# Where the last batch's x_proj is made: at the end of the first pass, or among the pieces of the scan pass

## The chip, the cores and the metric

The kernel runs on one core of one Trainium2 chip. The metric is the device time of one execution in microseconds (us); the median of a few runs counts. The profile is one execution, recorded instruction by instruction. Its engines are PE (matrix products and transposes, results in PSUM), PEld (PE's weight loads), DVE (vector), ACT (scalar, activation functions), POOL and SP, which here only starts transfers. Every engine works through its own list of instructions in order and waits on semaphores for the others.

## The reference, cut to what matters

A batch of 8 images of 64 x 64 points with 96 channels goes through a state-space block, a linear attention block and a feed-forward block. The change lies in the first of them:

```python
xz = jnp.einsum('bhwc,ec->bhwe', x, in_proj_w)         # 96 -> 384, split into xin, z
xc = jax.nn.silu(conv3x3_depthwise(xin) + conv_b)      # 192 channels: u
xs = concatenate([x_hwwh, flip(x_hwwh)], axis=1)       # 4 directions: rows, columns, both reversed
x_dbl = jnp.einsum('bkdl,kcd->bkcl', xs, x_proj_weight)   # x_proj: 192 -> 6 + 16 + 16
dts, Bs, Cs = split(x_dbl)
delta = jax.nn.softplus(einsum(dts, dt_projs_weight) + bias)
h = h * jnp.exp(d_t * A) + (d_t * u_t) * b_t           # the scan over L = 4096, 16 states
y = sum_n(h * c_t)
```

`x_proj` gives, for each point and direction, the 6 values that delta is made of, the 16 factors B and the 16 factors C. The scan of a batch can't start before that batch's x_proj is there.

## The kernel before, in words

There are three passes, each with tile pools of its own in SBUF and PSUM, which the next pass takes over; arrays go from pass to pass through HBM (`u_d`, `z_d`, `xd_d`, `b_d`, `dt_d`, `y_d`). The 8 batches are handled in four pairs. Of the 192 channels of two batches, three chunks of 128 are made (`chunk_rows`): the first 128 channels of each batch, and the last 64 of both together.

**First pass** (`pass1`). For each batch: statistics, projection (`projection`), a depthwise convolution of nine taps on DVE (`convolution`) into a tile `u` of 128 x 4096, SiLU on ACT. `u` is stored twice in `u_d`: row by row as it is (2 MB for a chunk) and, by way of ACT's copies `ut` (four of 128 x 1024, two buffers), column by column. `x_projection(b, o, q)` then makes x_proj of a batch for 512 points, for both directions of one order `o` at once: two products `px` of `u` with the weights `w_xp` (line 504), a copy from PSUM into `xd` (four buffers) by ACT, and a store into `xd_d`. There are 16 such units per batch. In the last batch every second copy is DVE's. `split` cuts the B and dt parts of `xd_d` into three bf16 parts (a load `bq`, ACT and POOL steps, two stores); for batches below `LATE` = 5 this is done in the first pass, for the others among the scans (`late_split`).

**Scan pass** (`pass2`). 192 pieces: pair, chunk, direction, quarter of 1024 points. `prepare` loads `xdt`, `xb` and `u` of a piece (for the very first piece on POOL's queue, for all others on SP's), and makes delta, `du` and transposes through the `wide` tiles in PSUM, of which there are three. Then for each of 16 states n: the decay `da` (ACT), the product `dbu` in a `wide` tile (by PE from ACT's or POOL's `x`, or from PE and a DVE product), the scan `h` (DVE, 2.3 us), and for every two states a product with C by POOL (`c`, loaded by SP into one of six buffers) and a sum by PE (`acc`).

**Third pass** (`pass3`): norm, gate, attention, feed-forward.

In each pass the order of instructions on each engine is written by a planner, `weave`. Units of work are generators that name the engine, an estimated cost and a delay; the planner takes, step by step, what can begin first, the lower rank where two can begin at once. It keeps `room` units of a kind open. `InOrder` (line 91 in the profile, for nearly every instruction) fixes that order. So a unit that is added shifts the order of others around it. The constants:

```python
LATE = 5
room = {"c": 6, "da": 3, "h": 3, "x": 3, "wide": 3, "xg": 1, "ud": 1, "acc": 1}
```

Of the kernel before, what the change touches and what calls it, by code (L numbers as in the profile page):

```python
# [33 lines left out]
F32 = mybir.dt.float32  # L34
# [8 lines left out]
P = 128  # L43
# [3 lines left out]
NXD = R + 2 * N  # L47
# [8 lines left out]
NS = 3  # L56

LATE = 5
GRP = 512
NG = L // GRP  # L60
RPG = GRP // WW
# [38 lines left out]
@with_exitstack  # L100
def vss_attn_ffn_kernel(ctx: ExitStack, tc: tile.TileContext, g: dict, out: bass.AP):
    nc = tc.nc
    consts = ctx.enter_context(tc.tile_pool(name="consts", bufs=1))
    dram = ctx.enter_context(tc.tile_pool(name="scratch", bufs=1, space=DRAM))

    ident = consts.tile([P, P], F32, name="ident")
    make_identity(nc, ident)
    mhalf = consts.tile([P, NBLK], F32, name="mhalf")
    nc.vector.memset(mhalf, -0.5)


    u_d = [[dram.tile([DI, L], F32, name=f"u_d{b}_{o}") for o in range(2)] for b in range(NB)]

    y_d = [[dram.tile([L, DI], F32, name=f"y_d{b}_{o}") for o in range(2)] for b in range(NB)]
    z_d = [dram.tile([DI, L], F32, name=f"z_d{b}") for b in range(NB)]
    xd_d = [[dram.tile([2 * NXD, L], F32, name=f"xd_d{b}_{o}") for o in range(2)] for b in range(NB)]

    b_d = [[dram.tile([2, NS, N, L], BF16, name=f"b_d{b}_{o}") for o in range(2)] for b in range(NB)]
    dt_d = [[dram.tile([2, NS, R, L], BF16, name=f"dt_d{b}_{o}") for o in range(2)] for b in range(NB)]

    engines = [InOrder(tc, e) for e in (nc.tensor, nc.vector, nc.scalar, nc.gpsimd)]
    fixed, load_dt_w = scan_constants(tc, g, consts, dram, ident)
    pass1(tc, g, load_dt_w, ident, mhalf, engines, u_d, z_d, xd_d, b_d, dt_d)
    pass2(tc, g, ident, engines, fixed, u_d, xd_d, b_d, dt_d, y_d)
    pass3(tc, g, ident, mhalf, engines, y_d, z_d, out)


# [138 lines left out]
def pass1(ctx, tc, g, load_dt_w, ident, mhalf, engines, u_d, z_d, xd_d, b_d, dt_d):  # L266
    nc = tc.nc
    pe, dve, act, pool = engines
    sp = InOrder(tc, nc.sync)
# [22 lines left out]
    conv_w = wp.tile([P, 2, 9], F32, name="conv_w")  # L292
    conv_b = wp.tile([P, 2, 1], F32, name="conv_b")

    w_xp = wp.tile([P, 3, 2, P], F32, name="w_xp")
    pool.memset(w_xp, 0.0)

    def later_loads():
# [191 lines left out]
    def x_projection(b, o, q):  # L490
        pair, j = b // 2, b % 2
        yield "u", pair, j
        yield "u", pair, 2
        px = None
        for ty, u in ((0, us[pair, j]), (1 + j, us[pair, 2])):
            end = yield ("pe", 0.62, 0.4) if px else ("pe", 0.62, 0.4, pxs)
            if px is None:
                px, slot = ps_px.tile([P, GRP], F32, name="px", tag="px"), pxs.taken
            if o == 0:
                src = u[:, q * GRP : (q + 1) * GRP]  # L500
            else:
# [10 lines left out]
        (dve.tensor_copy if by_dve else act.copy)(dst, src)  # L512
# [10 lines left out]
    for pair in range(NB // 2):  # L523
        batches = (2 * pair, 2 * pair + 1)
        for b in batches:
            units += [("stats", statistics(b, q)) for q in range(NG)]
            units.append(("norm", group_norm(b)))
            units += [("proj", projection(b, q)) for q in range(NG)]
        for c in ORDER:
            units.append(("conv", convolution(pair, c)))  # L530
        for b in batches:
            for o in range(2):
                units += [("xproj", x_projection(b, o, q)) for q in range(NG)]
                if b < LATE:
                    units += [("split", after(("xd", b, o), split((act, pool, sp), two, 4.4, xd_d[b][o], *w))) for w in splits(b, o, b_d, dt_d)]
# [3 lines left out]


@with_exitstack
def pass2(ctx, tc, g, ident, engines, fixed, u_d, xd_d, b_d, dt_d, y_d):
    nc = tc.nc
    KB = 2 * NS * N
    a_neg, dsum, dt_b, dt_w, sel, sel2 = fixed
# [27 lines left out]
    def prepare(at):  # L573
# [265 lines left out]
    for at, (pair, c, k, pc) in enumerate(pieces):  # L839
        by_act, by_pool = WAYS[c // 2]  # L840

        def add(kind, lead, unit, n=0):
            units.append((kind, at * N + n - lead, unit))

        add("prep", 8, prepare(at))
        for n in range(N):
            if n % 2 == 0:
                add("c", 12, load_c(at, n // 2), n)
            add("da", 2, decay(at, n), n)
            if n in by_act:  # L850
# [12 lines left out]
    units += [("split", 5 * N * (i + 1), late_split(*which)) for i, which in enumerate(last)]  # L863
    weave(units, {"prep": 1, "c": 1, "da": 2, "x": 1, "xg": 1, "dbu": 2, "scan": 2, "carry": 1, "term": 1, "sum": 1, "acc": 1, "split": 1}, done)


@with_exitstack
# [297 lines left out]
```

## Time and profile before

| | |
|---|---|
| median of 3 runs | 10121.8 us (10119.1 to 10127.6) |
| span of the profiled execution | 10130.1 us (its only listed time) |
| busy: DVE, ACT, POOL, PE | 9551 (94%), 9187 (91%), 8990 (89%), 7527 (74%) us |
| first convolution-free moment of DVE, last `px` product | 643.6 us, 695.2 us |
| first scan work on DVE | 716.6 us |
| one piece of the scan pass | about 44 to 46 us |
| scan pass | from about 710 to about 9300 us |
| granted clock of PE, mean | 0.906 |

An engine's busy share is a mean over three passes with different limits. In the timeline a line gives the start, the length, the engine and the operation, and in brackets how long the engine had been idle before it and what ended that. A piece's place in time is read here from the start of its product `du` on POOL, which every piece has once.

### The profile page before, as it was taken

What the parts mean: (1) busy time and instruction counts of PE and PEld (TensorE: products, weight loads), DVE (VectorE), ACT (ScalarE), POOL (GpSimd) and SP (SyncE); (2) the same over time, 40 slices, a digit from 0 to 9 for tenths busy, and PEclk for the clock granted to TensorE, in tenths of its full rate; (3) what the DMA queues carried; (4) which work ended last, traced back from release to release, by engine and by line L of the source; (5) the groups of instructions that cost most, each with busy time, mean ns of one, the idle gap of its engine ahead of it and who ended that gap; (6) DMA issues with size and microseconds to landing.
All of it is one profiled execution on the core that took longest, in us unless ns stands there. A gap on an engine that the chain in (4) does not pass through costs nothing.

```text
span 10130.1 us, 152413 instructions
## 1 busy us (share of the span) xinstructions
PE 7527.0 (74%) x52384; PEld 6235.5 (62%) x52384; DVE 9551.4 (94%) x7025; ACT 9186.9 (91%) x20692; POOL 8990.2 (89%) x2911
## 2 busy tenths in 40 slices
PE   7767777777777777777777777777777777776777
PEld 3336666665666666666666666655666666565666
DVE  7869999999999999999999999999999999998887
ACT  5669999999999999999999999999999999997776
POOL 1439999999999999999999999999999999998665
PEclk8889998989998989989999989999989999998887
DMA  5766776789976776799966766899767667998652
GB/s 167 233 205 215 225 236 217 229 210 206 209 219 213 225 218 214 223 211 200 223 211 214 230 212 223 212 205 209 217 213 225 218 212 224 208 203 183 192 151 77
DMA packets 932228, 2111.66 MB, mean 208 GB/s; under 512 B 274603, under 2 KB 422860, under 8 KB 929922
## 3 DMA queue, kind: packets, MB, share of 16 engines
q1 hardware_dynamic: 928650, 2100.57, 74.0%
q8 instruction: 419, 6.86, 0.3%
q14 instruction: 351, 2.88, 0.1%
q0 software_dynamic: 432, 0.94, 0.0%
q10 hardware_dynamic: 2376, 0.40, 0.0%
HBM read 1925.98 MB, written 175.66 MB: 207 GB/s over the span
## 4 chain that ended last, share of the span: by engine, by line
DVE 30%; ACT 29%; issue 15%; PE 13%; POOL 9%; DMA 3%; SPq 1%; DVEq 0%; ACTq 0%; POOLq 0%
DVE h L91 20%; ACT x L91 11%; ACT da L91 10%; POOL c L91 7%; PE acc L91 6%; DVE wide L91 5%; PE wide L91 3%; ACT L91 2%; ACT y L91 1%; POOL xg L91 1%; PE px L91 1%; PE pa L91 1%; ACT delta L91 1%; DMA xd_d<-xd 1%; DVE u L91 1%
## 5 line engine op out<-in xcount | busy, mean ns | idle before, releaser
L91 POOL TENSOR_TENSOR c<-c,h 128x2048 f32<-128x2048 f32 x1536 | 6959.5, 4557 | 300.0 <-issue 139.4
L91 DVE TENSOR_TENSOR_SCAN h<-da,carry,wide 128x1024 f32<-128x1024 f32 x2304 | 5268.3, 2332 | 137.5 <-PE wide L91 36.8
L91 ACT ACTIVATE x<-duT,bT 128x128 f32<-128x128 f32 (+1 forms) x13312 | 3970.8, 369 | 2.0
L91 PE MATMUL acc<-ident,c 128*128 128x128 f32 x24576 | 3439.1, 298 | 571.0 <-POOL c L91 563.3
L91 ACT ACTIVATE da<-delta,a_neg 128x1024 f32<-128x1024 f32 x3072 | 3513.4, 1144 | 316.2 <-DVE h L91 303.1
L91 PEld LDWEIGHTS acc<-ident,c 128*128 128x128 f32 x24576 | 3123.4, 155 | 1005.5 <-POOL c L91 891.2
L91 PE MATMUL wide<-ident,x 128*128 128x128 f32 x10752 | 1560.7, 291 | 645.3 <-DVE h L91 586.4
L91 PEld LDWEIGHTS wide<-ident,x 128*128 128x128 f32 x10752 | 1306.9, 150 | 841.5 <-ACT x L91 399.4
L91 DVE TENSOR_TENSOR_SCAN h<-da,wide 128x1024 f32<-128x1024 f32 x768 | 1712.9, 2271 | 46.2 <-PE wide L91 14.0
L91 DVE TENSOR_TENSOR wide<-du,wide 128x1024 f32<-128x1024 f32 x1280 | 1544.0, 1208 | 39.9 <-PE wide L91 39.6
L91 PE MATMUL wide<-xb,sel 96*128 96x512 bf16 x2560 | 820.5, 404 | 697.4 <-DVE h L91 686.4
L91 POOL TENSOR_TENSOR xg<-duT,bT 128x512 f32<-128x512 f32 (+1 forms) x640 | 894.5, 1414 | 28.3 <-PE wide L91 15.2
L91 PEld LDWEIGHTS <-sel 96*128 96x128 bf16 x2560 | 232.7, 102 | 878.1 <-DVE h L91 626.3
L91 PE MATMUL wide<-ident,xg 128*128 128x128 f32 x3584 | 483.8, 279 | 119.0 <-DVE h L91 116.4
L91 ACT ACT_TABLE_LOAD x386 | 495.2, 1283 | 26.3 <-DMA w_qT<-in_WqT_b 19.5
L91 PEld LDWEIGHTS wide<-ident,xg 128*128 128x128 f32 x3584 | 412.6, 144 | 148.9 <-issue 111.2
L91 POOL TENSOR_TENSOR du<-delta,u 128x1024 f32<-128x1024 f32 x192 | 457.5, 2383 | 7.5 <-ACT delta L91 7.5
L91 DVE SCALAR_TENSOR_TENSOR u<-xpad,conv_w,u 128x4096 f32<-128x4096 f32 x96 | 450.9, 4697 | 1.9
L91 PE MATMUL px<-u,w_xp 128*128 128x512 f32 x512 | 252.7, 633 | 63.4 <-ACT u L91 43.8
L91 POOL TENSOR_TENSOR gt<-gt,zs 128x512 f32<-128x512 f32 x128 | 161.8, 1275 | 132.1 <-ACT gt L91 111.9
L91 ACT COPY y<-acc 128x1024 f32<-128x1024 f32 x192 | 192.6, 1003 | 83.8 <-PE acc L91 83.5
L91 POOL TENSOR_TENSOR bq<-bq,bs 128x512 f32<-128x512 f32 (+1 forms) x48 | 115.1, 2400 | 166.9 <-ACT bs L91 155.1
(142 smaller groups left out, 5987.7 us busy)
## 6 DMA issues: line engine op xcount, KB each, us to landing
c<-xd_d SPq DMA_DIRECT2D x1024, 1024.0 KB
c<-xd_d SPq DMA_DIRECT2D x1024, 512.0 KB
u<-u_d SPq DMA_DIRECT2D x127, 512.0 KB
xdt<-dt_d SPq DMA_DIRECT2D x1146, 36.0 KB
xb<-b_d SPq DMA_DIRECT2D x382, 96.0 KB
u<-u_d SPq DMA_DIRECT2D x128, 256.0 KB
zs<-z_d SPq DMA_DIRECT2D x128, 256.0 KB
y_d<-y SPq DMA_DIRECT2D x24, 1024.0 KB
```

The source lines that it names most:

```text
L91: ins = getattr(self.engine, op)(*args, **kwargs).ins
```

## The change

For batches from `LATE_X` = 7 on, so for the last batch alone, `x_projection` is no longer put into the first pass. In its place, sixteen units `late_x_projection` are put into the scan pass. Each loads 512 points of `u` (or of its column order) back from `u_d` into a tile `ux` (three transfers), makes the two products into a `wide` tile, copies it with ACT into a tile `xd` and stores it in `xd_d`. One such unit is open at a time. The late splits of batch 7 wait for them. `w_xp` lies in a pool of its own that both passes share, so that other tiles of the passes lie at other addresses.

```diff
+LATE_X = 7
...
-    pass1(tc, g, load_dt_w, ident, mhalf, engines, u_d, z_d, xd_d, b_d, dt_d)
-    pass2(tc, g, ident, engines, fixed, u_d, xd_d, b_d, dt_d, y_d)
+    with tc.tile_pool(name="shared", bufs=1) as shared:
+        w_xp = shared.tile([P, 3, 2, P], F32, name="w_xp")
+        pass1(tc, g, load_dt_w, ident, mhalf, engines, w_xp, u_d, z_d, xd_d, b_d, dt_d)
+        pass2(tc, g, ident, engines, fixed, w_xp, u_d, xd_d, b_d, dt_d, y_d)
...
-        by_dve = b == NB - 1 and q % 2 == 1
-        end = yield ("dve" if by_dve else "act"), 0.6 if o == 0 else 0.8
+        end = yield "act", 0.6 if o == 0 else 0.8
...
-            for o in range(2):
+            for o in range(2 if b < LATE_X else 0):
...
+    def late_x_projection(b, o, q):
+
+        yield "scans", 0
+        pair, j = b // 2, b % 2
+        cols = slice(q * GRP, (q + 1) * GRP)
+        yield "sp", 1.8, 4.0
+        ux = one.tile([P, 2, GRP], F32, name="ux")
+        sp.dma_start(ux[:, 0, :], u_d[b][o][0:P, cols])
+        for i in range(2):
+            sp.dma_start(ux[64 * i : 64 * i + 64, 1, :], u_d[2 * pair + i][o][P:DI, cols])
+        yield "pe", 1.5, 0.2, slots["wide"]
+        px, slot = take("wide", [P, T])
+        for i, ty in enumerate((0, 1 + j)):
+            pe.matmul(px[:, 0:GRP], w_xp[:, ty, o, :], ux[:, i, :], start=i == 0, stop=i == 1)
+        end = yield "act", 0.58, 0.2
+        xd = one.tile([2 * NXD, GRP], F32, name="xd")
+        act.copy(xd, px[0 : 2 * NXD, 0:GRP])
+        slots["wide"].release(slot, end)
+        end = yield "sp", 0.7, 3.0
+        sp.dma_start(xd_d[b][o][:, cols], xd)
+        one_more(("xd", b, o), NG, end)
...
     def late_split(b, o, which):
 
         yield "scans", 0
+        if b >= LATE_X:
+            yield "xd", b, o
...
+    late_x = [(b, o, q) for b in range(LATE_X, NB) for o in range(2) for q in range(NG)]
+    units += [("late", 3 * N * (i + 1), late_x_projection(*which)) for i, which in enumerate(late_x)]
     last = [(b, o, w) for b in range(LATE, NB) for o in range(2) for w in splits(b, o, b_d, dt_d)]
     units += [("split", 5 * N * (i + 1), late_split(*which)) for i, which in enumerate(last)]
-    weave(units, {"prep": 1, ..., "acc": 1, "split": 1}, done)
+    weave(units, {"prep": 1, ..., "acc": 1, "late": 1, "split": 1}, done)
```

More of the change, by code (lines that the diff above doesn't have):

```diff
@@ L265, in pass1 @@
 @with_exitstack
-def pass1(ctx, tc, g, load_dt_w, ident, mhalf, engines, u_d, z_d, xd_d, b_d, dt_d):
+def pass1(ctx, tc, g, load_dt_w, ident, mhalf, engines, w_xp, u_d, z_d, xd_d, b_d, dt_d):
     nc = tc.nc
@@ L293, in pass1 @@
     conv_b = wp.tile([P, 2, 1], F32, name="conv_b")
-    w_xp = wp.tile([P, 3, 2, P], F32, name="w_xp")
     pool.memset(w_xp, 0.0)
@@ L511, in x_projection @@
             src, dst = src.rearrange("p (h w) -> p w h", w=RPG), xd.rearrange("p (w h) -> p w h", w=RPG)
-        (dve.tensor_copy if by_dve else act.copy)(dst, src)
+        act.copy(dst, src)
         pxs.release(slot, end)
@@ L541, in pass2 @@
 @with_exitstack
-def pass2(ctx, tc, g, ident, engines, fixed, u_d, xd_d, b_d, dt_d, y_d):
+def pass2(ctx, tc, g, ident, engines, fixed, w_xp, u_d, xd_d, b_d, dt_d, y_d):
     nc = tc.nc
@@ L861, in pass2 @@
         add("acc", 0, take_acc(at), N)
+    late_x = [(b, o, q) for b in range(LATE_X, NB) for o in range(2) for q in range(NG)]
+    units += [("late", 3 * N * (i + 1), late_x_projection(*which)) for i, which in enumerate(late_x)]
     last = [(b, o, w) for b in range(LATE, NB) for o in range(2) for w in splits(b, o, b_d, dt_d)]
     units += [("split", 5 * N * (i + 1), late_split(*which)) for i, which in enumerate(last)]
-    weave(units, {"prep": 1, "c": 1, "da": 2, "x": 1, "xg": 1, "dbu": 2, "scan": 2, "carry": 1, "term": 1, "sum": 1, "acc": 1, "split": 1}, done)
+    weave(units, {"prep": 1, "c": 1, "da": 2, "x": 1, "xg": 1, "dbu": 2, "scan": 2, "carry": 1, "term": 1, "sum": 1, "acc": 1, "late": 1, "split": 1}, done)
 @with_exitstack
```

## The prediction

> **What bounds the kernel now.** I read four views, from wide to narrow. The page's forty slices say where engines rest.
>
> ```profile
> DVE  7869999999999999999999999999999999998887
> ACT  5669999999999999999999999999999999997776
> POOL 1439999999999999999999999999999999998665
> ```
>
> Each slice is 253 us. From the fourth slice to the 36th all three are nine tenths busy or more: that is the scan pass. The third slice (507 to 760 us) holds the seam between the passes, which the change edits. The busy time by stretches takes it apart (columns: stretch, its length, then busy us and instructions of PE, PEld, DVE, ACT, POOL, the granted clock, the DMA share, GB/s).
>
> ```profile
> 660.00:680.00 20.00, 15.85 (x33) 6.10 (x32) 2.75 (x4) 7.65 (x7) 0.00 (x0) 0.91 0.58 174
> 680.00:700.00 20.00, 13.17 (x26) 4.98 (x24) 1.37 (x2) 1.75 (x3) 3.88 (x8) 0.91 0.53 193
> 700.00:710.00 10.00, 1.24 (x10) 0.37 (x10) 1.37 (x2) 2.08 (x3) 0.99 (x2) 0.50 0.81 260
> ```
>
> ```profile
> 888.00:1953.00 1065.00, 805.11 (x5930) 698.28 (x5931) 1028.20 (x528) 1027.59 (x2244) 1047.26 (x296) 0.92 0.70 224
> 3046.00:4100.00 1054.00, 807.86 (x5952) 690.99 (x5950) 1030.70 (x529) 1014.67 (x2212) 1012.15 (x264) 0.92 0.69 218
> ```
>
> DVE's last convolution ends at 643.6 us and its first scan work begins at 716.6; between, it does eight copies of 0.69 us. So the seam costs 73 us in which nobody is bound by arithmetic. The two rows of the second fence are the same 24 pieces of the scan pass (fifth to 28th of a pair), in the first pair, with late splits among them, and in the second, without. The timeline of the seam, picked from several engines' answers, gives the order of events (start, length, engine, operation; in brackets the idle time before it and its releaser).
>
> ```profile
> 658.52 2.58 SPq L91 DMA_DIRECT2D u_d<-ut  x1
> ...
> 668.55 1.92 ACT L91 COPY ut<-u 128x1024 f32<-128x1024 f32 x1 [5.78 <-DMA u_d<-ut]
> ...
> 684.74 1.44 SPq L91 DMA_DIRECT2D u_d<-u  x1
> ...
> 696.12 3.27 POOL L91 DMA_DIRECT2D xdt<-dt_d  x6 [36.22 <-PE px L91]
> 699.38 1.03 POOL L91 DMA_DIRECT2D xb<-b_d  x2
> ...
> 708.04 0.36 PE L91 MATMUL wide<-sel,xb 96*128 96x16 bf16 x8 [12.24 <-DMA xd_d<-xd]
> ...
> 716.60 2.36 DVE L91 TENSOR_TENSOR wide<-du,wide 128x1024 f32<-128x1024 f32 x2 [9.49 <-PE wide L91]
> ```
>
> POOL held the loads of the first piece for 36.2 us, until the last x_proj product (px) of batch 7 was over: `xdt` takes SBUF that the first pass gives back only then. PE's first scan product then waited 12.2 us, until the last store of an `xd` had let DVE make the last copy (706.4 to 707.1); `xb`, issued at 699.4 and 7.7 us on its way, came at the same moment. Last, the waits of DVE in the two long stretches, first pair and then second.
>
> ```profile
> DVE h L91 <- PE wide L91: 14.1, 15, 2.4
> DVE wide L91 <- PE wide L91: 6.6, 7, 1.1
> ```
>
> ```profile
> DVE wide L91 <- PE wide L91: 4.1, 4, 1.1
> DVE h L91 <- PE wide L91: 3.7, 6, 1.2
> ```
>
> In the scan pass DVE is the bound (1030.7 of 1054 us), POOL and ACT rest for 42 and 39 us of it, and almost all that DVE waits for are PE's tiles in the three `wide` buffers.
>
> **The sum's base.** The span is 10130.1 us; no other time is listed for that execution. The median of the runs, 10121.8, lies 8.3 lower. I carry differences over to the median unscaled.
>
> **What is removed: the tail.** Sixteen units of batch 7 go: 32 matmuls of 0.59 us, 16 copies of 0.58 or 0.69, 16 stores of 152 KB. Little of this is a sum of busy times; what counts is what is last without them. In the changed program `xdt` waits only for the last convolution and an older product, both over by 643.6, so POOL can issue it after its last split step, at 659.9. The next gate is `xb` (and the first `c` load): in the changed program it waits for the pass's last store, `u_d<-u` of 2 MB, and for the last `ut` copy. So the question is when that store goes.
> - The first `ut` store is issued at 658.5 and was landed at 668.5, when the third copy began: 10.0 us. I leave that.
> - The second `ut` copy stood behind an `xd` copy and its store behind two `xd` stores (issue at 665.5). Without them the copy runs from 658.7 to 660.7, and the store goes at about 661. At 10.0 us each, the fourth copy starts at 671, ends at 673, and the 2 MB store goes at 674 instead of 684.7.
> - That store took until about 694: the DMA rate is 270 GB/s from 684.7 to 694 and 90 GB/s from there to 700. So 9.3 us, and landing at 683.3.
> - `xb` then goes at 683.3 instead of 699.4: 16.1 us earlier. From there to PE's first product lay 8.7 us.
>
> Against this: the six first `c` loads (1 MB each), which had to let `xd` stores pass (one went at 698, five from 707.4), are now all released by the same landing as `xb`. I take 2 us for that, and 14 us of gain. Bounds: if the 2 MB store goes no earlier, `xb` still goes at 694, 5.4 us gained, and with its 7.7 us doubled by the `c` loads 2.3 us are lost; if `ut` stores take 6 us instead of 10, 20 us are gained.
>
> The Trainium skill, "DMA: Bandwidth & Descriptors", section "Issuing engines are not separate DMA queues", says that transfers started by different engines share the same 16 DMA engines and interleave; it speaks against the change, since POOL's queue will not shield `xb` from SP's `c` loads. The page's section "Anatomy of one DMA" puts a DMA of this path at 2.0 us plus bytes over 436 GB/s, which would make 2.2 us of the 96 KB of `xb`, as an estimate; the row has 7.7. By that figure the gain would be nearer 20 us than 14. The sum goes by the row.
>
> **What is added: sixteen late units.** In the changed order their matmuls stand in pieces 2 to 17, about one per piece.
> - SP: three loads and a store per unit, at the 450 ns of an `xd` store 1.8 us, 29 us over some 700. SP mostly waits for free `c` buffers, six deep; that is the cover. A store that waits for ACT's copy holds up the `c` loads behind it, again covered by those buffers.
> - DMA: 664 KB per unit, 10.6 MB in all. The share is 0.70 at 224 GB/s, so 320 GB/s full: 33 us of transfers in some 210 us of free DMA time. Hidden; 33 us if that cover were gone. The product stands 0.1 to 1.9 pieces behind its load, over 4 us, so PE should not wait for it; the nearest case, the `bq` loads of the late splits, made ACT wait once, 2.0 us.
> - PE: 2 x 0.59 us, 19 us in all, of 246 us that PE is idle in 24 pieces. Hidden.
> - ACT: 16 x 0.58 = 9.3 us beside 37 us of idle time. Hidden in total, not always in place.
> - The `wide` buffer: the unit takes one of three, and in ACT's order the copy that frees it stands one to four scans behind the product, mostly two. Meanwhile DVE's products turn on two buffers.
>
> No row shows such a unit. From above: each costs DVE one scan, 2.33 us, 37 us together. From below: the same 24 pieces take 1054.3 us in the second pair and 1057.7 in the third and fourth, so order alone moves 3 us, and -3 is possible. The nearest row is the late splits: 16 of them lie in the first pair's 24 pieces, which take 1065.5 us, 8.9 over the mean of the others (1056.6): 0.56 us each, for 2.36 us of POOL and 1.2 of ACT. The new unit has none of the POOL work, the closest engine behind DVE, so I take 0.45: 7 us.
>
> **What moves: the late splits.** Not in the diff, but in the changed order: their last POOL step stands in piece 18.6 instead of 24.6. The 24 pieces hid 16 x 2.36 - 8.9 = 28.9 us of split work, 1.2 per piece; six pieces fewer hide 7 us less at most. I take 3. From the 28th piece on, the orders of all compute engines are the same.
>
> **Sum.** -14 + 7 + 3 = -4: span 10126, median 10118.
>
> **The rivals.** First, *the late units cost a scan each*: DVE finds only two `wide` buffers and loses a scan time per unit. 16 x 2.33 + 3 - 14 = +26, 10148. For it: nearly all of DVE's waiting is on `wide`. Against: every piece makes three such detours already (`bT`, `delta`, `duT`), and DVE waits 7.8 us in 24 pieces, 0.11 per detour. It decides from 2.0 us a unit on.
> Second, *tail gone, units free*: quicker `ut` stores, units in DVE's existing gaps, splits unharmed. -20 - 3 = -23, 10099. For it: 73 us of seam; against: the stores of `u` stay, and they are 6 MB issued between 650 and 686.
> Third, *it does not shorten the seam*: the stores were the real gate and go no earlier: -5.4 + 10 = +5, 10126. It would be inside what cannot be told from no change.
>
> **How the numbers follow.** About 0.2%, 20 us, is what a measurement of this kernel can tell from no change. The forecast (net between -20 and +20, the third rival included at 0.15) has 0.78; the first rival 0.11, the second 0.11. The range 10102 to 10138 leaves out both rivals' far halves and takes in a gain of 5 to 20 with a cost of 1 to 22.
>
> **What would show it.** Right: no px after 650 us; POOL's `xdt` near 660; `xb` at 680 to 687; DVE's first scan work at 700 to 706; the fifth to 28th piece at 1070 to 1080 us; everything after that unchanged to 3 us. Wrong: DVE waiting for `wide` over 50 us in that stretch (first rival); `xb` still at 694 or later (third); a stretch under 1066 (second).

## The result, and the profile after

| | before | after |
|---|---|---|
| median of 8 runs each | 10112.98 us (10109.1 to 10127.6) | 10140.81 us (10131.7 to 10148.3) |
| ratio | | 1.0024, interval 1.0014 to 1.0033 |
| span of the profiled execution | 10130.1 us | 10146.5 us |

The change makes the kernel slower by 0.24%, some 28 us by the medians and 16.4 by the two profiled executions (that of before lies high, with 10130.1 in span, where the median of its eight runs is 10113). The forecast was 4 us less, its range ended at 10138, and the chance given to "slower" was 0.11.

I took both traces apart at the starts of the product `du` on POOL, one per piece (pieces counted from 0; `xb` is the time of its issue).

| | `xb` | piece 0 begins | pieces 0 to 32 | 32 to 191 | after that |
|---|---|---|---|---|---|
| before | 699.4 | 711.3 | 1416.6 | 7139.8 | 862.4 |
| after | 680.4 | 691.6 | 1459.7 | 7136.7 | 858.5 |
| difference | -19.0 | -19.7 | +43.1 | -3.1 | -3.9 |

So -19.7 + 43.1 - 3.1 - 3.9 = +16.4: a gain at the seam, larger than I had said, and a loss of 43 us in the first pair's first 32 pieces, where I had said 10. The views of before, asked again. First the busy tenths:

```profile
DVE  7879899999999999999999999999999999998887
ACT  5669899999999999999999999999999999997776
POOL 1449999999999999999999999999999999998665
```

The third digit of DVE and POOL went up: work starts sooner. The fifth digit of DVE and ACT, 1015 to 1268 us, fell from 9 to 8, in the midst of the scan pass. The timeline of the seam, picked from several engines' answers:

```profile
659.59 3.27 POOL L92 DMA_DIRECT2D xdt<-dt_d  x6
...
672.85 0.37 SPq L92 DMA_DIRECT2D u_d<-u  x1
...
680.41 1.03 POOL L92 DMA_DIRECT2D xb<-b_d  x2 [17.55 <-DMA u_d<-u]
...
688.41 0.36 PE L92 MATMUL wide<-sel,xb 96*128 96x16 bf16 x8 [43.52 <-issue]
...
696.94 2.36 DVE L92 TENSOR_TENSOR wide<-du,wide 128x1024 f32<-128x1024 f32 x2 [52.59 <-PE wide L92]
```

POOL's first loads no longer wait for a product; they stand right behind its last split step. `xb` waits for the 2 MB store, as the prediction said, and DVE's first scan work comes 19.7 us earlier. Then the waits of DVE in the fifth to 28th piece, which now last from 868.6 to 1977.5 us (a line gives the total, the number of waits and the longest):

```profile
DVE h L92 <- PE wide L92: 37.5, 24, 4.0
DVE wide L92 <- PE wide L92: 12.2, 14, 2.7
DVE h L92 <- ACT da L92: 7.8, 7, 2.4
```

Before, these were 14.1, 6.6 and 0.5. The busy time of that stretch and of the same pieces of the second pair (columns as in the prediction):

```profile
868.60:1977.50 1108.90, 837.70 (x6006) 709.38 (x6004) 1035.68 (x530) 1037.77 (x2257) 1047.61 (x297) 0.91 0.68 223
```

```profile
3068.50:4121.40 1052.90, 802.12 (x5955) 690.75 (x5952) 1030.45 (x529) 1014.55 (x2213) 1012.33 (x266) 0.93 0.68 218
```

DVE has 530 and 529 operations in the two and is busy for nearly the same time, 1036 and 1030 us, but takes 56 us more: it is idle, not slowed. Of the 43 us that the first pair's stretch lost against before, 29 are waits for PE's `wide` tiles (49.7 us against 20.7) and 7 waits for ACT's decay `da`, while PE itself is busy for only three quarters of the time.

### The profile page after: what moved, and what is told of

Its sections match the earlier page's. It is cut to its first block, busy times and chain, and to the rows that moved or that the text cites. A ratio compares the mean times of both kernels' runs of the same rounds, so it can differ in the third digit from the quotient of the medians.

```text
span 10146.5 us, 152464 instructions
## 1 busy us (share of the span) xinstructions
PE 7509.6 (74%) x52384; PEld 6221.6 (61%) x52384; DVE 9550.1 (94%) x7017; ACT 9192.3 (91%) x20700; POOL 8995.7 (89%) x2911
## 5 line engine op out<-in xcount | busy, mean ns | idle before, releaser
L92 POOL TENSOR_TENSOR xg<-duT,bT 128x512 f32<-128x512 f32 (+1 forms) x640 | 893.1, 1411 | 30.3 <-PE wide L92 16.4
L92 ACT ACT_TABLE_LOAD x386 | 495.2, 1283 | 26.5 <-DMA w_qT<-in_WqT_b 19.7
L92 PE MATMUL wide<-ident,du 128*128 128x128 f32 x1536 | 206.6, 278 | 64.9 <-DVE h L92 33.7
```

Source lines behind the costliest of these rows:

```text
L92: ins = getattr(self.engine, op)(*args, **kwargs).ins
```

## The experiments

"First 32" is the stretch of pieces 0 to 32 in the profiled execution; where all the late work is gone it takes 1417.5 us. An engine's *list* is the order of its instructions in the scan pass, the late units' own left out. Two executions whose lists agree on PE, ACT, POOL and DVE (after and e15_hold) differ in that stretch by 3.0. The stretch is read from one execution each: by the ratios to before, which go over many, e7_slot, e11_pe and e18_order lie 7 to 9 us above e1_fill, where the stretch gives 2 to 5. The stretch from piece 32 to 191 took between 7136.0 and 7143.1 us in all the kernels whose units lie in the first pair, so that what counts is in the first 32 pieces.

### The gain at the seam

**e1_fill.** Each of the sixteen units becomes one store:

```diff
-        sp.dma_start(ux[:, 0, :], u_d[b][o][0:P, cols])
...
-        end = yield "sp", 0.7, 3.0
-        sp.dma_start(xd_d[b][o][:, cols], xd)
+        end = yield "sp", 0.7, 30.0
+        sp.dma_start(xd_d[b][o][:, cols], xd_d[b - 1][o][:, cols])
```

> The late units make no x_proj: each copies 512 points of batch 6's x_proj into batch 7's place within HBM (so batch 7's scan works on batch 6's delta, B and C). No product, no wide buffer, no ACT copy, no load of u. All theories of the units' price expect the gain of the seam alone: first scan work of DVE near 697 us as in the changed kernel, the fifth to 28th piece as in the kernel before (1060 to 1068 us), net -18 to -22 us against before. If the 24 pieces stay above 1085 us, the price lies in the planner's shifted order or in the transfers, and not in the units' compute.

Measured: ratio 0.9984 (0.9975 to 0.9993), `xb` at 681.5, first 32 at 1417.5. The seam's gain is there alone, about 0.16%. In the scan pass this kernel's lists on PE, ACT, POOL and DVE are those of before, the late splits' places among them (up to piece 26, where after has them up to piece 20), and the first 32 pieces take what they took (1416.6). So the loss comes with the units or with the lists that they bring; e18_order parts the two.

**e4_ring.** From before: the tile `xd` of batch 7 comes from three pools in turn, so that products wait less for their stores.

```diff
-        xd = four.tile([2 * NXD, GRP], F32, name="xd")
+        if b == NB - 1:
+            xd = (four, four, three)[q % 3].tile([P if q % 3 == 2 else C if q % 3 == 1 else 2 * NXD, GRP], F32, name=("xd", "xn", "z0")[q % 3])[0 : 2 * NXD]
+        else:
+            xd = four.tile([2 * NXD, GRP], F32, name="xd")
```

> The kernel before, all of x_proj in the first pass, but the xd copies of batch 7 go to eleven buffers instead of four: those of xn and z0, idle by then, are taken in turn with those of xd. No late units. If the stores of xd, which ACT and DVE wait for, make the tail, the last product comes at about 670 us instead of 695, the last copy at 672, and xb waits for the 2 MB store of u alone, which goes some 5 to 8 us earlier: first scan work of DVE at 703 to 710 us, net -7 to -14 us, the rest as before. If the DMA engines and not the number of buffers make the tail, it stays at 714 to 717, net 0 to -3.

**e10_first.** The same, and the last chunk's store of `u` (2 MB) stands ahead of the `ut` stores.

```diff
+        if last:
+            yield "sp", 0.5
+            for part, b, ch in parts:
+                sp.dma_start(u_d[b][0][ch, :], u[part, :])
...
+        if not last:
             for part, b, ch in parts:
                 sp.dma_start(u_d[b][0][ch, :], u[part, :])
```

> No late units: the kernel with x_proj in the first pass and eleven buffers for batch 7's xd, and in the very last chunk the 2 MB row store of u is issued before the four ut copies instead of after them. If the landing of that store is the seam's last gate, xb goes at 686 to 692 us instead of 698, first scan work of DVE at 702 to 708, net -8 to -15 us against before. If the stores of xd and ut, pushed behind it, become the last ones, first scan work stays at 712 to 717 and net is 0 to -4.

Measured: 0.9993 (0.9983 to 1.0002) and 0.9999 (0.9990 to 1.0009), neither to be told from no change. The timeline of POOL shows why, e4_ring's first:

```profile
684.89 3.27 POOL L91 DMA_DIRECT2D xdt<-dt_d  x6 [26.44 <-PE px L91]
698.28 1.03 POOL L91 DMA_DIRECT2D xb<-b_d  x2 [10.12 <-DMA u_d<-u]
```

```profile
693.94 3.27 POOL L91 DMA_DIRECT2D xdt<-dt_d  x6 [27.06 <-PE px L91]
697.20 1.03 POOL L91 DMA_DIRECT2D xb<-b_d  x2
```

In e4_ring the products end 11 us sooner and POOL then waits for the store of `u`; in e10_first that wait is gone, and the products end late again. Two gates lie a few us apart; with the products left in the first pass, opening one shows the other.

### What the price of the units depends on

**e2_narrow.** Products of 64 columns instead of 512, which ACT's copy reads eight times over; all else in place.

```diff
-            pe.matmul(px[:, 0:GRP], w_xp[:, ty, o, :], ux[:, i, :], start=i == 0, stop=i == 1)
+            pe.matmul(px[:, 0:64], w_xp[:, ty, o, :], ux[:, i, 0:64], start=i == 0, stop=i == 1)
```

**e3_twice.** Both products are made twice.

```diff
-        for i, ty in enumerate((0, 1 + j)):
+        for i, ty in [*enumerate((0, 1 + j)), *enumerate((0, 1 + j))]:
```

> The two products of each late unit are made for 64 of the 512 points alone, and ACT copies these 64 columns eight times over (so x_proj of batch 7 is right for every eighth block only). Loads, wide buffer, size of the ACT copy, store and order stay as in the changed kernel; PE's time per unit falls from 2.0 to 3.8 us to about an eighth. Theory 1 (PE's time in a row makes DVE's tiles late): the 24 pieces fall from 1109 us to 1070 to 1080, net -5 to +5 us against before. Theory 2 (a wide buffer is withheld until ACT's copy): they stay at 1095 to 1109, net +15 to +24. Theory 3 (the late splits, drawn together into 18 pieces, overload POOL): the same as theory 2, but with POOL and not PE in front of DVE's waits.

> The two products of each late unit are made twice over, the second time over the first; the order is otherwise that of the changed kernel, and the splits lie in the same pieces. Theory 1: 16 more times 2.0 to 3.8 us of PE in a row, the 24 pieces rise from 1109 to 1140 to 1165 us, net +55 to +80 us against before. Theory 2: the wide buffer is withheld by some 6 us per unit before and 9 now, the pieces rise to 1120 to 1130, net +35 to +45. Theory 3: no change beyond 5 us, net +20 to +30.

Measured: e2_narrow 1.0006 (0.9996 to 1.0015), first 32 at 1441.7; e3_twice 1.0045 (1.0030 to 1.0060), 1474.2. The lists of the three kernels are the same on PE, ACT, POOL and DVE. PE's time for all units is 12.8 us in e2_narrow, 43.9 in after, 72.0 in e3_twice; the prices over e1_fill are 24.2, 42.2 and 56.7. The price rises with PE's time, by 0.5 to 0.6 us for each of PE, but more than half of it stays when the products are short.

**e5_loads, e6_act, e7_slot, e11_pe.** Parts of the unit alone: e5 has the loads and a store of `ux`; e6 the loads and ACT's copy (from `ux`); e7 the loads, short products and the turn of a `wide` buffer, which is back when PE is through; e11 is e7 with the full products.

The edit of e5 (products and copy are left out), of e6 (products are left out) and of e11 (copy is left out; e7 has `px[:, 0:64]` and `ux[:, i, 0:64]` besides):

```diff
-        yield "pe", 1.5, 0.2, slots["wide"]
...
-        slots["wide"].release(slot, end)
         end = yield "sp", 0.7, 3.0
-        sp.dma_start(xd_d[b][o][:, cols], xd)
+        sp.dma_start(xd_d[b][o][:, cols], ux[0 : 2 * NXD, 0, :])
```

```diff
-        yield "pe", 1.5, 0.2, slots["wide"]
...
-        act.copy(xd, px[0 : 2 * NXD, 0:GRP])
-        slots["wide"].release(slot, end)
+        act.copy(xd, ux[0 : 2 * NXD, 0, :])
```

```diff
-        yield "pe", 1.5, 0.2, slots["wide"]
+        end = yield "pe", 1.5, 0.2, slots["wide"]
...
-        end = yield "act", 0.58, 0.2
-        xd = one.tile([2 * NXD, GRP], F32, name="xd")
-        act.copy(xd, px[0 : 2 * NXD, 0:GRP])
         slots["wide"].release(slot, end)
         end = yield "sp", 0.7, 3.0
-        sp.dma_start(xd_d[b][o][:, cols], xd)
+        sp.dma_start(xd_d[b][o][:, cols], ux[0 : 2 * NXD, 0, :])
```

> The late unit loads its 512 points of u as in the changed kernel and stores 76 rows of them as if they were x_proj (so batch 7's delta, B and C are values of u). No product, no wide buffer, no ACT copy. Its 48 loads and 16 stores come within the third and fourth piece. If the transfers have a price (SP's queue, the DMA engines), the pieces 2 to 18 rise above the 708 to 711 us of the kernel before and of the filled one, by up to 10; if they have none, net -18 to -22 us against before.

> As the one with the loads alone, and ACT's copy of 76 x 512 from the loaded u (from SBUF instead of PSUM) stands between load and store. No product, no wide buffer. If ACT's 9.3 us fall into its idle time, net -16 to -21 us against before; if they count in full, -9 to -12.

> The unit loads u, takes a wide buffer for its two products of 64 columns, gives it back when PE is done, and stores rows of u as x_proj. No ACT copy behind the product. PE takes 13 us for all units as in the narrow kernel. If it is the wait for ACT's copy that withholds the buffer, the price of the narrow kernel (+25 us in the first 32 pieces, net +5) falls to that of 13 us of PE at the slope of the dose series, 0.56, so 7 us: net -15 to -10. If a turn of the wide buffers is lost anyhow, net 0 to +5.

> As the unit that gives the wide buffer back when PE is done (no ACT copy; rows of u are stored as x_proj), but with the products in full, 44 us of PE instead of 13. The late splits reach piece 24.6 in both. If PE's time in a row has the price of the dose series (0.56 us per us), the first 32 pieces rise from 1420 to 1434 to 1440 us, net +3 to +9. If the price is mostly the buffer withheld until ACT has copied, they stay below 1428 and net is -12 to -5.

Measured: e6_act 0.9986 (0.9977 to 0.9996), first 32 at 1421.3; e7_slot 0.9991 (0.9982 to 1.0000), 1419.9; e11_pe 0.9991 (0.9981 to 1.0000), 1419.2. So copies alone cost 3.8 us, turns of a buffer with short products 2.4, and turns with full products, 40.0 us of PE in that execution, 1.7. None of these parts has the price by itself. e7_slot and e11_pe have one and the same lists, so in these 29 us more of PE cost nothing that can be told. But the lists are not after's: they differ from the third piece on.

e5_loads, with the least work of all, was slow: 1.0044 (1.0029 to 1.0058), first 32 at 1468.4. Its waits of SP's queue and of PE from 691 to 2000 us:

```profile
SPq L92 <- DMA xd_d<-ux: 93.9, 15, 10.7
```

```profile
PE wide L92 <- DMA xb<-b_d: 60.6, 2, 31.9
```

Its stores read what a load has just been told to bring, and on SP's queue they stand close behind it. Each holds the queue until the load has landed, and PE waited for the `xb` of two pieces behind them, for 28.7 and 31.9 us. This is that kernel's own trouble, not the price sought: e7_slot and e11_pe have such stores too (e11_pe 113.5 us of these waits from 770 to 1500 us) at next to no price, because there no `xb` is late.

**e8_spread.** The units begin with the second pair, one to every second piece.

```diff
-        yield "scans", 0
+        yield "scans", 48 + 2 * (o * NG + q)
```

> The changed kernel in full, but unit i may begin only after the scans of piece 48 + 2i, in the second pair, where it meets no late splits of batches 5 and 6; those of batch 7 follow to piece 83. The correct x_proj is made. If the price is PE's time and the buffer's turn, wherever they fall, the 32 pieces from 48 on rise by 35 to 45 us and net is +15 to +25. If the meeting of units and late splits makes half of it (POOL and ACT full with both), they rise by 15 to 25 and net is -5 to +5.

Measured: 1.0026 (1.0016 to 1.0036). Its first 32 pieces take 1408.3 us, but pieces 48 to 80, where the units now are, take 1431.9 (1405.6 before) and 80 to 96 take 747.9 (739.8 before). The price goes where the units go. Batch 7's six late splits went with them, and the first 32 pieces are 9 us shorter than in e1_fill, so over pieces 0 to 191 the profiled execution is 24.8 us longer than e1_fill's, against 37.7 in after. That execution is the fastest of its ten, though, and the medians (1.0026 here, 1.0024 in after) show nothing saved by half as many units per piece.

**e9_gate.** The late splits are held back, split i until 1.35 i pieces are through; the units stay.

```diff
-    def late_split(b, o, which):
+    def late_split(b, o, which, i):
 
-        yield "scans", 0
+        yield "scans", int(1.35 * i)
```

> The changed kernel in full, but the late split i may begin only after the scans of piece 1.35 i, so that the 18 splits spread to piece 25.6 as in the kernel before, instead of 20. The units lie in pieces 2 to 18 as they did. If the price of the units is in part that of the splits drawn together (POOL full), the first 32 pieces fall from 1460 us to 1440 to 1447, net +3 to +10 us against before. If the units alone carry it, they stay at 1455 to 1462, net +17 to +24.

Measured: 1.0032 (1.0020 to 1.0044), first 32 at 1460.9 against 1459.7. Spreading the splits does not lower the price, with the units standing at other places in the lists.

### Is it the held buffer?

A buffer is taken by PE and given back by ACT's copy; where PE gives it back (e7, e11) the price was gone, though in other lists. So my theory by now was the held buffer, and its rival the store, which holds SP's queue until the copy is over.

**e12_eight.** Eight units of twice the size: four products into the whole `wide` tile, one copy of 76 x 1024, one store. **e13_actstore, e16_eight_act.** The store goes by ACT's queue, with sixteen and with eight units. **e14_lag.** The planner is told that the copied `xd` is ready 12 us later, so the store stands further back in SP's list. **e15_hold.** As after, but SP stores from `ux` and so waits for no copy.

The core of e12 (e16 has it too):

```diff
-        cols = slice(q * GRP, (q + 1) * GRP)
+        cols = slice(2 * q * GRP, 2 * (q + 1) * GRP)
...
-        for i, ty in enumerate((0, 1 + j)):
-            pe.matmul(px[:, 0:GRP], w_xp[:, ty, o, :], ux[:, i, :], start=i == 0, stop=i == 1)
+        for h in range(2):
+            for i, ty in enumerate((0, 1 + j)):
+                half = slice(h * GRP, (h + 1) * GRP)
+                pe.matmul(px[:, half], w_xp[:, ty, o, :], ux[:, i, half], start=i == 0, stop=i == 1)
...
-        act.copy(xd, px[0 : 2 * NXD, 0:GRP])
+        act.copy(xd, px[0 : 2 * NXD, :])
```

e13 (and e16), e14 and e15:

```diff
-        end = yield "sp", 0.7, 3.0
-        sp.dma_start(xd_d[b][o][:, cols], xd)
+        end = yield "act", 0.1, 3.0
+        act.dma_start(xd_d[b][o][:, cols], xd)
```

```diff
-        end = yield "act", 0.58, 0.2
+        end = yield "act", 0.58, 12.0
...
-        slots["wide"].release(slot, end)
+        slots["wide"].release(slot, end - 11.8)
```

```diff
-        sp.dma_start(xd_d[b][o][:, cols], xd)
+        sp.dma_start(xd_d[b][o][:, cols], ux[0 : 2 * NXD, 0, :])
```

> Eight late units of 1024 points instead of sixteen of 512: the same products, PE time and bytes, half the turns of a wide buffer, half the ACT copies (of 76 x 1024) and half the transfers. The correct x_proj is made. If the price goes by turns of the buffer, the first 32 pieces fall from 1460 us to 1437 to 1445, net 0 to +8. If it goes by PE's time, now 4 to 7.6 us in a row, they stay at 1455 to 1470, net +18 to +32.

> The changed kernel in full, but ACT's queue and not SP's starts the store of xd, right behind its copy. If SP's queue is the price (the store waits there for ACT's copy and loads behind it come late), the first 32 pieces fall from 1460 us to 1418 to 1432, net -18 to -5 us against before. If it is the wide buffer held until ACT's copy, they stay at 1450 to 1465, net +12 to +25.

> The changed kernel in full, but the planner is told that xd is ready 12 us later, so the store stands some three scans further back in SP's order and should no longer wait there. SP's queue as the price: 1420 to 1435 us in the first 32 pieces, net -15 to 0. The held buffer as the price: 1450 to 1465, net +12 to +25.

> Products, wide buffer and ACT copy as in the changed kernel, but the store takes rows of the loaded u (so batch 7's delta, B and C are values of u) and does not wait for ACT's copy. The held buffer as the price: the first 32 pieces stay at 1450 to 1462 us, net +12 to +24. SP's queue as the price: 1418 to 1430, net -18 to -6.

> Eight late units of 1024 points with their store on ACT's queue; the correct x_proj is made. With eight units and the store on SP the first 32 pieces take 1423 us. SP's queue as the price: 1416 to 1421, net -12 to -18 us against before. The held buffer: 1421 to 1427, net -5 to -12.

| | ratio, interval | first 32 | over e1_fill |
|---|---|---|---|
| e12_eight | 0.9992 (0.9983 to 1.0002) | 1422.9 | +5.4 |
| e13_actstore | 1.0015 (1.0006 to 1.0024) | 1447.9 | +30.4 |
| e14_lag | 1.0009 (1.0000 to 1.0018) | 1442.7 | +25.2 |
| e15_hold | 1.0029 (1.0017 to 1.0041) | 1456.7 | +39.2 |
| e16_eight_act | 1.0007 (0.9998 to 1.0016) | 1433.6 | +16.1 |

e15_hold, in after's lists, keeps nearly the whole price with SP's wait for the copy gone: that wait is not the cause. (Its stores wait for loads instead, 91.7 us from 770 to 1500 us; in e11_pe that wait, 113.5, was harmless.) e13_actstore and e14_lag, in which the planner also puts the units elsewhere, keep 30 and 25 us, and e16_eight_act is dearer than e12_eight: ACT's queue is no better place for the store. e12_eight does the same products in eight units and costs 5.4 us (they took PE 31.2 us there, against 43.9 in after). It holds each buffer longer than any kernel with sixteen units (6.8 us at the mean, PE's start to the copy's end, against 4.7 in after), eight times instead of sixteen. It fits the held buffer only if the number of turns counts as well. So the theory needed a direct test.

**e17_apart.** Sixteen full products and sixteen copies and the store behind them, but the copy reads `ux`: the buffer is free when PE is through.

```diff
-        yield "pe", 1.5, 0.2, slots["wide"]
+        end = yield "pe", 1.5, 0.2, slots["wide"]
...
+        slots["wide"].release(slot, end)
         end = yield "act", 0.58, 0.2
         xd = one.tile([2 * NXD, GRP], F32, name="xd")
-        act.copy(xd, px[0 : 2 * NXD, 0:GRP])
-        slots["wide"].release(slot, end)
+        act.copy(xd, ux[0 : 2 * NXD, 0, :])
```

> Everything of the sixteen units stays as in the changed kernel (three loads, two full products into a `wide` tile, an ACT copy of 76 x 512 into `xd`, a store of `xd` that waits for that copy), except that the copy reads `ux` and not the products, so the `wide` buffer is free when PE is through with it (the results of x_proj of the last batch are left out). Held-buffer theory: the price is that of the parts done singly, 1.7 us for the full products alone and 3.8 for the copies alone, so the first 32 pieces take 1417.5 + 5.5 = 1423 us, 1418 to 1429, and the time is 10105 to 10117. Rival, that full products and copies and stores together crowd PE, ACT and SP whoever holds the buffer: the price of the changed kernel stays for the most part, first 32 pieces 1445 us or more, the time 10135 or more.

Measured: 1.0016 (1.0006 to 1.0026), first 32 at 1450.8, or 33.3 over e1_fill. The theory falls: of 42.2 us at most 8.9 go with the hold until the copy, and 33.3 stay without it.

**e18_order.** The other way about: every step of the units stays in the planner, turns and all, so that the other instructions stand in after's order in the scan pass; loads, products and copies are not issued.

```diff
         yield "pe", 1.5, 0.2, slots["wide"]
         px, slot = take("wide", [P, T])
-        for i, ty in enumerate((0, 1 + j)):
-            pe.matmul(px[:, 0:GRP], w_xp[:, ty, o, :], ux[:, i, :], start=i == 0, stop=i == 1)
         end = yield "act", 0.58, 0.2
-        xd = one.tile([2 * NXD, GRP], F32, name="xd")
-        act.copy(xd, px[0 : 2 * NXD, 0:GRP])
         slots["wide"].release(slot, end)
         end = yield "sp", 0.7, 3.0
-        sp.dma_start(xd_d[b][o][:, cols], xd)
+        sp.dma_start(xd_d[b][o][:, cols], xd_d[b - 1][o][:, cols])
```

> The sixteen units keep every step of the changed kernel in the planner, with the same costs, delays and turns of a `wide` buffer, so that all other instructions of the scan pass stand in the same order on every engine as in the changed kernel; but the loads, the products and ACT's copy are not issued, and only the fill of e1_fill is (x_proj of the last batch is left out). If the price is the units' own work (PE's products, ACT's copies, what waits for them): the first 32 pieces take 1417.5 us give or take 6, the time 10095 to 10108, like e1_fill. If it is the order into which the planner shifts the rest: the price of e2_narrow, whose products are short and whose order is this one, stays for the most part: first 32 pieces 1435 us or more, the time 10115 or more. Between: both, in the share that is seen.

Measured: 0.9993 (0.9984 to 1.0003), first 32 at 1422.0, or 4.5 over e1_fill. The lists by themselves, the bunched late splits among them, cost little. DVE's waits from 770 to 1500 us, for e18_order, e17_apart and after:

```profile
DVE h L92 <- PE wide L92: 14.5, 12, 6.7
DVE wide L92 <- PE wide L92: 5.4, 3, 4.0
```

```profile
DVE h L92 <- PE wide L92: 33.1, 19, 3.8
DVE wide L92 <- PE wide L92: 10.2, 9, 4.0
```

```profile
DVE h L92 <- PE wide L92: 36.2, 21, 4.0
DVE wide L92 <- PE wide L92: 10.1, 11, 2.7
```

e18_order, e2_narrow, after and e3_twice have the same lists on PE, ACT, POOL and DVE to the last instruction, so they give the parts of the price: 4.5 us for the lists (e18_order); 19.7 more with short products, loads, copies and the held buffer (e2_narrow, 24.2); 18.0 more when the products have full length (after, 42.2); 14.5 more when they are made twice (e3_twice, 56.7). e17_apart's lists are the same up to piece 15. At that piece's start after is 29.1 us behind e18_order, and e17_apart 25.5: there the freed buffer has saved 3.6 us, hardly more than two executions with one list differ by. The other 5.3 of the 8.9 came after the lists had parted.

### Where a unit stands

That leaves the question why the products cost next to nothing in e11_pe. There the planner, with no ACT step to place, made other lists for these engines and put the units elsewhere in PE's. One unit of after, picked from the timelines of DVE, PE and ACT:

```profile
1157.51 1.21 DVE L92 TENSOR_TENSOR wide<-du,wide 128x1024 f32<-128x1024 f32 x1
1157.64 3.78 PE L92 MATMUL wide<-ux,w_xp 128*128 128x512 f32 x4 [1.63 <-DVE h L92]
1158.85 2.35 DVE L92 TENSOR_TENSOR_SCAN h<-da,carry,wide 128x1024 f32<-128x1024 f32 x1
1161.22 3.09 PE L92 MATMUL acc<-ident,c 128*128 128x128 f32 x16
1161.46 0.58 ACT L92 COPY xd<-wide 76x512 f32<-76x512 f32 x1 [1.52 <-PE wide L92]
1164.14 1.04 PE L92 MATMUL wide<-ident,x 128*128 128x128 f32 x8
1165.22 2.35 DVE L92 TENSOR_TENSOR_SCAN h<-da,carry,wide 128x1024 f32<-128x1024 f32 x1 [4.03 <-PE wide L92]
```

The bracket of the product says that PE had waited 1.63 us for a scan of DVE to give a buffer back: none was free. DVE had one filled tile left. The freed buffer went to the unit, not to the next scan's product; PE makes the unit (3.78 us), then the sums that stand next (3.09), then the tile that DVE waits for. The one scan in hand lasts 2.35 us, and DVE is idle for 4.03. Neither ACT's copy nor the hold decides here: PE is busy without a gap until the tile.

But 3.78 and 3.09 us are not what these steps always take. In e15_hold, whose lists are the same, the same unit reads:

```profile
1155.68 1.98 PE L92 MATMUL wide<-ux,w_xp 128*128 128x512 f32 x4 [1.63 <-DVE h L92]
1157.50 1.91 PE L92 MATMUL acc<-ident,c 128*128 128x128 f32 x16
1159.25 1.04 PE L92 MATMUL wide<-ident,x 128*128 128x128 f32 x8
1160.33 2.35 DVE L92 TENSOR_TENSOR_SCAN h<-da,carry,wide 128x1024 f32<-128x1024 f32 x1 [1.09 <-PE wide L92]
```

In the busy times over the two units, after's first, the column behind POOL's differs, the granted clock: 0.50 and 1.00.

```profile
1157.64:1161.42 3.78, 3.78 (x5) 1.61 (x6) 3.42 (x2) 2.30 (x5) 3.78 (x2) 0.50 0.02 4
```

```profile
1155.68:1157.66 1.98, 1.98 (x6) 0.97 (x7) 1.85 (x2) 1.98 (x5) 1.98 (x1) 1.00 0.04 8
```

At full clock the unit and the sums are through in 3.6 us instead of 6.5, and DVE is idle for 1.1 us instead of 4.0. In these traces the granted clock is either 1.00 or 0.50, in steps of 3.41 us.

I added up DVE's waits in the 10 us behind the start of each unit's product. In after, the eight units that ran wholly at clock 1.00 have 7.9 us of them, 1.0 each; the eight that ran at 0.50 in part or whole have 24.3, 3.0 each. In e11_pe it is 4.3 us for eleven (0.4 each) and 13.5 for five (2.7); in e17_apart 9.9 for eleven (0.9) and 15.3 for five (3.1). Whether the product had first waited over 1 us for a scan, as eleven did in after, makes little difference there at full clock: 1.1 each for the four that had, 0.9 for the four that had not. The sixth to ninth unit stand at the same places of the same lists in after, e15_hold and e17_apart; the four passages at full clock have 0.2 to 1.4 us behind them, the eight at a lowered clock 1.7 to 4.0. So the clock of the moment goes with what a unit costs, more than its place alone. This is a comparison of traces, not an experiment.

What lowers the clock was not tested, but the trace of after has a sign. From 770 to 1500 us it falls 26 times, and in the step just before PE had been busy for 34% at the mean, in 25 of the 26 for less than half. Of the 149 steps at 1.00 that were followed by another at 1.00, PE was busy for 78% at the mean, and for less than half in 7. So a stretch in which PE mostly stands and waits for buffers is often followed by a lower clock, and a unit that comes then runs slowly.

All this is not the whole price. From 770 to 1600 us DVE waits for 20.4 us in before, 23.9 in e1_fill, 28.5 in e18_order, 30.7 in e11_pe, 58.0 in e17_apart and 64.1 in after. Of the 35.6 us between e18_order and after, with the same lists, 24.7 lie in the 10 us behind the units, 10.9 elsewhere. Of the 33.4 between e11_pe and after, 14.4 lie behind the units and 19.0 elsewhere, so e11_pe's lists are better for more than the units. And the number of units at a lowered clock does not foretell the price of a kernel: it is five in e11_pe, e17_apart and e9_gate, with 1.7, 33.3 and 43.4 us. What else makes up the difference stays open. So does the rest of e2_narrow's price, whose products are short (0.6 to 2.0 us a unit); its loads and copies were not parted from the hold in that order.

No version with all the work beats before for certain. e12_eight comes nearest, at 0.9992 (0.9983 to 1.0002), DVE's first scan work comes 20.5 us sooner there (696.1) and the first 32 pieces take 6.3 longer than before (1422.9 against 1416.6): the 14 us that are left can hardly be told from no change.

## Why the prediction was wrong

**The step that failed** is "What is added: sixteen late units". I took 0.45 us a unit, 7 us in all. The first 32 pieces became 42.2 us longer (after less e1_fill), of which 37.7 are the units' own work (after less e18_order, with the same lists), 2.4 each. I had chosen the late splits as nearest row, 0.56 us each. But those take POOL's and ACT's time and no `wide` buffer, and "almost all that DVE waits for are PE's tiles in the three `wide` buffers" stood in my own text. The bound from above, a scan of 2.33 us for each unit, 37 in all, was the near one. That it fits so closely is luck in part: the units do not cost a scan each. The price rises with the length of the products (e2_narrow, e3_twice), and DVE's waits behind a unit are 1.0 us at full clock and 3.0 at a lowered one.

**The first rival** had the sign and nearly the time: 10148 with 2.33 a unit, where 10141 was measured; its mark, DVE waiting for `wide` over 50 us in the fifth to 28th piece, is just short at 49.7 (37.5 + 12.2), and its point of decision, 2.0 us a unit, was passed. Its mechanism is right in part: the unit takes the buffer that DVE's next tile needs. That the buffer is then held until ACT's copy was the part that I had stressed in the text, and it is worth at most 8.9 us of 42.2 (e17_apart). I gave it 0.11 because `bT`, `delta` and `duT` already take such turns cheaply. Turns as such are cheap in e7_slot and e11_pe, 2.4 and 1.7 us for sixteen, even with 2.0 to 3.8 us of PE in each. In after's lists, with ACT's copy behind the product, they are not: with short products sixteen cost 19.7 (e2_narrow less e18_order), and the length adds the rest.

**PE's time for a unit** was mis-sized: 2 x 0.59 us, 19 us in all. The trace has two records for each of these products:

```profile
L92 PE MATMUL wide<-ux,w_xp x64: 590/697/1222, 785.0 to 1496.2; 128*128 128x512 f32 x64
```

64 records for 32 products, of 0.59 to 1.22 us: a unit takes 1.9 us at best and 3.8 at worst, 43.9 in all. The shortest records run at a granted clock of 1.00, the longest at 0.50. The row of before, with 512 records of `px` for 256 products, would have told it. "Hidden" was wrong by more than size: 246 us of idle PE in 24 pieces say nothing on a gap of one scan. Nor was it quite right that PE should not wait for the loads: one product of after waited 4.45 us for its `ux`.

**The seam** was right in its order and short in size: 19.7 us earlier instead of 14. The last store went at 672.85 (I said 674) and landed at 680.4 (683.3), and `xb` followed at once. The 2 us that I set aside for the `c` loads were not needed: from `xb` to PE's first product lay 8.0 us, against 8.7 before, with a DMA share of 0.91 from 680 to 700. The Trainium skill, "DMA: Bandwidth & Descriptors", section "Issuing engines are not separate DMA queues", says that transfers from different queues interleave on the same 16 DMA engines; that is no contradiction, but here the row shows no delay from it.

**The late splits** were to cost 3 us. e18_order has them as bunched as after and is 4.5 us above e1_fill, which has them where before has; that fits, but it takes in all of the other order too. e9_gate shows no gain from spreading them. **"Unchanged to 3 us"** for the rest held: 7136.7 against 7139.8. **Right marks:** no `px` after 650 us (the last at 644.9), `xdt` at 659.6, `xb` at 680.4. **Wrong marks:** DVE's first scan work at 696.9, not 700 to 706, and the fifth to 28th piece at 1108.9, not 1070 to 1080.

**The second rival** needs free units; e1_fill, which has the units' work taken away, gains 0.16%, 16 us, where the rival had 23. **The third**, that the stores are a gate of their own, holds for before with faster products (e4_ring), not for the change, which lets the stores go earlier too.

By terms, in the profiled executions: -19.7 (seam) + 37.7 (units) + 4.5 (order, splits among it) + 0.9 (e1_fill less before) - 7.0 (the rest of the span) = +16.4, where the prediction had -14 + 7 + 3 = -4.

## What to carry to other kernels

Idle time of an engine in a stretch does not hide work that lands in its list between a released buffer and the tile that the bound engine waits for: price such work by the depth of the stock (here one scan, 2.35 us) against what stands in line ahead of the next tile, and at the clock that PE has at that moment. For a unit that takes a turn of a shared buffer, take its nearest row from things that take that turn with as much work of the same engine, and multiply by the number of units, before counting shares. Fewer, larger units can cost much less than many small ones with the same arithmetic: eight cost 5.4 us (e12_eight) and 16.1 (e16_eight_act), sixteen 42.2. And compare lists before times: where they agree on every engine, kernels show what a step costs, where the lists differ, the step is not parted from its place.

## What the runs showed of the chip that I had not expected

An f32 product of 128 x 128 by 128 x 512 is two records on PE. A record takes 0.59 us where the granted clock is 1.00 and 1.06 where it is 0.50 (the first of a unit 0.67 to 0.70, and 1.22), and both clocks stand side by side, in steps of 3.41 us, in a stretch whose mean is 0.91; the price of a late unit varies with the moment. Transfers on SP's queue wait in line: one store that depends on the load just ahead of it held the queue for up to 10.7 us, and PE then waited 31.9 us for a load behind it (e5_loads). The Trainium skill, "Perfetto Trace Analysis", section "Optimization Strategy", says that gaps which recur on the engine that should be saturated can mean too few PSUM buffers for the next tile. Here the gaps recur and end with a `wide` tile in PSUM, but the number of turns was the same in e7_slot, e11_pe and after, with 2.4, 1.7 and 42.2 us: with as many buffers and turns, the order of the lists, ACT's copy and PE's clock make the difference.
